# Four graph-attention layers over a sparse list: the order in which a group's rows and a dense block's heads are summed on TensorE

## The chip, the core and the metric

One NeuronCore of a Trainium2 chip runs the whole program; the other cores are idle. The metric is the device time of one execution in microseconds. Three executions of the kernel before took 2966.52, 2974.07 and 2981.21 us, median 2974.07.

A core has engines with queues of their own that meet only through semaphores: TensorE (PE; its loads of the stationary operand are listed as PEld), VectorE (DVE), ScalarE (ACT), GpSimd (POOL) and SyncE (SP, which here only issues DMAs). An instruction may carry an increment of its engine's semaphore, which happens when the instruction has ended, and instructions of other engines wait for a value of it.

## The reference

The input is 3327 nodes with 512 features in f32 and a symmetric adjacency matrix of about half a per cent density with a full diagonal. Four graph-attention layers follow each other, with 8, 4, 1 and 8 heads. Each is a normalization, a projection, a softmax over a node's neighbours and a weighted sum of their projected features, added to the node's own features. Layer 0, cut to its core:

```python
h = maximum(layernorm(x), 0)
v = (h @ W.T).reshape(n, H, d)                 # H heads of d = 512 / H columns
e = leaky_relu(e_src[:, None, :] + e_dst[None, :, :], 0.2)   # e_src, e_dst: v times two vectors a head
e = where(mask[:, :, None], e, -inf)
alpha = softmax(e, axis=1)
x = x + einsum('ijh,jhd->ihd', alpha, v).reshape(n, H * d)
```

Layers 1 and 2 put an ELU on the sum before they add it. All layers use the same adjacency.

## The kernel before

The nodes are padded to 26 tiles of 128. A first stage, the build, finds each node's neighbours (at most 40), sorts the nodes by degree and writes for each tile of 128 nodes (in order of degree) the indices of up to CAPS[t] neighbours, 36 for the first tile down to 11 for the last.

A layer then goes over its tiles, from the smallest degree to the largest. Tile t has CAPS[t] rows a node; they are taken in groups of up to four (GROUP). The rows are fetched by `Tile.fetch` (L836): POOL issues one indirect DMA for each row, which gathers 128 table rows of 528 values into a buffer g. There are five such buffers, so gathers run up to five groups ahead.

`Tile.scored` makes a group's weights on DVE (L893 and L895, or L915 and L917; in layer 0 with an exponential on ACT, L896). `Tile.group` multiplies and sums. For each row q of the group DVE writes the product of row and weights (L941), 128 by 512 f32, into row q of a buffer m; there are five of those. The tile's very first row is written straight into the tile's PSUM bank `po` instead. TensorE then adds the rows of m to the bank, one matmul with the identity for each (L946). An f32 matmul is two passes on TensorE, so each is two MATMUL and two LDWEIGHTS records. Layer 2 has one head and sums on DVE (L932 and L934), without these matmuls. Two banks `po` alternate between tiles.

When a tile's groups are done, its sum is divided (`means`, L964), up to four groups later, and added to x (L984), normalized (L992 to L1000), transposed on TensorE (L451), cut to positive values by ACT (L458), projected by TensorE (L469), and scaled and written to the next layer's table (L476 and L1031, a DMA from SP).

The first tiles, whose nodes have the most neighbours, are taken as dense blocks in layers 1, 2 and 3 (1, 9 and 3 tiles, DENSE): there all 26 tiles of source nodes are read in turn, with a mask. Layer 2's block is `Wholes` (L1192 is its matmul). Layers 1 and 3 use `Several`: for each of 52 units (two halves of the heads by 26 source tiles), SP loads features and mask (L1284, L1285), ACT makes ramps of the scores into PSUM (`weights`, L1298) and the scaled features vs of each of Q heads (`features`, L1309 and, for a last column, L1310), DVE adds and masks (L1314) and writes the weights e, and TensorE sums (`products`, L1332), one matmul for each of n tiles and Q heads: 2 in layer 1, 12 in layer 3. There are two buffers of e, two of vs, and one PSUM buffer of the ramps.

In `tile_gat_lists` all of this is put in an order by hand: a layer is a sequence of steps, one for each group, and each piece of work is put down with `later` for the start ("first"), the middle ("scored") or the end ("last") of a step. POOL, PE, DVE and ACT run their instructions in the order in which they are written. The framework adds the semaphores: an instruction waits only where it needs a value that its engine has not yet seen, and an increment is left off an instruction that nobody waits for (a later one then adds several at once).

The bank's sum does not depend on the order of its rows but for rounding, and the dense block's heads go to places of their own.

Of the kernel before, what the change touches and what calls it, by code (L numbers as in the profile page):

```python
# [374 lines left out]
def twice(ap, gap):  # L375

    return bass.AP(tensor=ap.tensor, offset=ap.offset,
                   ap=[list(ap.ap[0]), [gap, 2], list(ap.ap[-1])])
# [419 lines left out]
def tile_gat_lists(ctx: ExitStack, tc: tile.TileContext, x, adj, ws, avs, out, ident, half, slots, L, low, spare, mine, tabx, tabs):  # L798
# [7 lines left out]
    nc = tc.nc  # L806
# [40 lines left out]
    class Tile:  # L847
# [72 lines left out]
        def group(self, i):  # L920


            H, K, wt = HEADS[self.l], CAPS[self.t], self.wt
            D = F // H
            k0, n, g = self.groups[i]
            if H == 1:
                for q in range(n):
                    v = g[:, q, :].rearrange("p (s m) -> p s m", s=2)[:, :, :F // 2]
                    acc = self.po.rearrange("p (s m) -> p s m", s=2)
                    w = wt[:, k0 + q, 0:1]  # L930
                    if k0 + q == 0:
                        nc.vector.tensor_scalar(acc, v, w, None, OP.mult)  # L932
                    else:
                        nc.vector.scalar_tensor_tensor(acc, v, w, acc, OP.mult, OP.add)  # L934
                return
            m = pools["m"].tile([P, GROUP, F], F32, name="m")
            for q in range(n):
                v = g[:, q, :].rearrange("p (s m) -> p s m", s=2)[:, :, :F // 2]

                out_ = self.po if k0 + q == 0 else m[:, q, :]  # L940
                nc.vector.tensor_tensor(out_.rearrange("p (s h d) -> p s h d", s=2, d=D),  # L941
                                        v.rearrange("p s (h d) -> p s h d", d=D),
                                        wt[:, k0 + q, :H].rearrange("p (s h) -> p s h", s=2)
                                        .unsqueeze(3).to_broadcast([P, 2, H // 2, D]), OP.mult)
            for q in range(k0 == 0, n):
                nc.tensor.matmul(self.po, ident, m[:, q, :], start=False, stop=(k0 + q == K - 1),  # L946
                                 skip_group_check=True)

        def divisors(self):
# [176 lines left out]
    class Wholes:  # L1126
# [59 lines left out]
        def products(self, p, j):  # L1186
            e, v = self.e.pop((p, j)), self.v.pop((p, j))
            for q in range(3):
                tl = self.tiles[3 * p + q]
                if j == 0:  # L1190
                    tl.po = pools["w"].tile([P, BANK], F32, name="whole")
                nc.tensor.matmul(tl.po.rearrange("p (s m) -> p s m", s=2), e[:, q * P:(q + 1) * P],  # L1192
                                 v.rearrange("p (s m) -> p s m", s=2)[:, :, :F // 2],
                                 start=(j == 0), stop=(j == NT - 1))
# [51 lines left out]
    class Several:  # L1246
# [70 lines left out]
        def products(self, u):  # L1317

            Q, DV = self.Q, self.DV
            j, e, vs = u % NT, self.e[u % 2], self.vs[u % 2]  # L1320
            if j == 0:
                self.po = [pools["w"].tile([P, BANK], F32, name="whole") for _ in range(0, self.n * Q, self.per)]
                for o in self.po:
                    nc.tensor.matmul(o, ident, zero.to_broadcast([P, BANK]), start=True, stop=False,
                                     skip_group_check=True)
            for q in range(self.n):
                for h in range(Q):
                    o, o0 = self.where(q, h)
                    dst, mov = o[:, o0:o0 + DV], vs[:, h * DV:(h + 1) * DV]
                    if self.H == 8:  # L1330
                        dst, mov = twice(dst, self.per * DV - o0), twice(mov, (Q - h) * DV)
                    nc.tensor.matmul(dst, e[:, h, q * P:(q + 1) * P], mov, start=False, stop=(j == NT - 1),  # L1332
                                     skip_group_check=True)
# [169 lines left out]
```

## Time and profile before

| | us |
|---|---|
| median of three executions | 2974.07 |
| the profiled execution | 2992.93 |
| its span, from the first to the last instruction | 2991.2 |
| build (to the first matmul of L946) | 315 |
| layer 0 | 805 |
| layer 1 | 720 |
| layer 2 | 460 |
| layer 3 | 692 |

Mean granted TensorE clock: 0.862 of full speed. Busy shares over the span: PE 75%, PEld 42%, DVE 64%, ACT 31%, POOL 58%. The layers' times are stretches of the span between the first and the last matmul of L946 of each, rounded.

How to read the lines that follow. A group of instructions is its line, engine, operation, what it writes and reads with shapes, its count; then busy time and the mean of one in ns; then the idle time of the engine just before such instructions and what ended it. In a table of waits: who waited, for what; us in total, times, longest. "issue" is idle time in which the engine waited for nothing that the profile shows; "remote", in the chain "another core or an unknown queue", is a wait on a semaphore whose update the profile cannot put down to an instruction that ended shortly before. In a timeline: start, us, engine, line, operation, count, and in brackets the idle time before it.

Some of the other groups, for comparison:

| line, engine | what | count | mean ns |
|---|---|---|---|
| L836 POOL | one gather of 128 rows, by the second list of indices | 712 | 954 |
| L469 PE | projection of a tile, one pass | 1664 | 420 |
| L1192 PE | dense block of layer 2, one pass | 468 | 651 |
| L1314 DVE | add and mask, layer 3 | 35 of its kind | 1755 |
| L1309 ACT | features of one head, layer 3 | 136 of its kind | 338 |

### The profile page before, as it was taken

How to read it: one execution, taken by the hardware profiler on the slowest of the kernel's cores; microseconds unless marked ns; L12 is line 12 of the kernel's file. 1: busy time of each engine (PE TensorE's matmuls, PEld its weight loads, DVE VectorE, ACT ScalarE, POOL GpSimd, SP SyncE). 2: the span in 40 equal slices, each digit the busy share in tenths (PEclk: the TensorE clock that was granted, in tenths of full speed). 3: DMA queues.
4: the chain of work that ended last, by engine and by line, in shares of the span. 5: the costliest groups of instructions: out<-in, count | busy, mean ns of one | idle time of the engine just before them, and what ended most of it. 6: DMA issues, size and time to landing. Idle time of an engine off the chain costs nothing.

```text
span 2991.2 us, 26834 instructions
## 1 busy us (share of the span) xinstructions
PE 2235.0 (75%) x7082; PEld 1251.2 (42%) x7082; DVE 1901.9 (64%) x4831; ACT 919.9 (31%) x2363; POOL 1728.8 (58%) x1717
## 2 busy tenths in 40 slices
PE   4777687677677745788878787779785778777777
PEld 2665243343333322444434444345444445444443
DVE  7887656555555523776756655787776556656565
ACT  5782123322221111332222222343333333233230
POOL 7885455465456664565555552666664555545554
PEclk9888788888788877898888898989897888888889
DMA  6885477677676666676666664878765666656654
GB/s 229 308 288 170 136 223 212 183 233 219 184 208 188 199 179 180 189 206 185 201 207 188 195 188 122 248 242 260 222 215 148 192 189 189 178 169 183 182 171 137
DMA packets 258856, 594.16 MB, mean 199 GB/s; under 512 B 101827, under 2 KB 119235, under 8 KB 254342
## 3 DMA queue, kind: packets, MB, share of 16 engines
q0 software_dynamic: 124368, 432.13, 49.1%
q1 hardware_dynamic: 130582, 153.43, 16.3%
q10 hardware_dynamic: 3744, 6.82, 0.7%
q8 instruction: 57, 0.93, 0.1%
q14 instruction: 105, 0.86, 0.1%
HBM read 542.58 MB, written 49.65 MB: 198 GB/s over the span
## 4 chain that ended last, share of the span: by engine, by line
PE 28%; DVE 15%; issue 15%; another core or an unknown queue 8%; ACT 4%; POOL 3%; DMA 3%; SPq 0%; DVEq 0%; POOLq 0%; ACTq 0%
PE bank L946 17%; DVE m L941 6%; PE whole L1332 5%; PE pv L469 3%; POOL g L836 3%; PE whole L1192 2%; DVE bank L934 2%; DMA g<-tab,idxb 1%; DVE x L984 1%; DVE q L439 1%; DMA g<-tab,idxa 1%; DVE pw L917 1%; DMA ve<-tab 1%; DVE z L915 0%
## 5 line engine op out<-in xcount | busy, mean ns | idle before, releaser
L946 PE MATMUL bank<-m,ident 128*128 128x512 f32 x2414 | 1243.7, 661 | 279.9 <-issue 122.8
L836 POOL DMA_INDIRECT g<-tab,idxb x712 | 679.1, 954 | 488.0 <-issue 193.5
L946 PEld LDWEIGHTS bank<-m,ident 128*128 128x128 f32 x2414 | 490.0, 211 | 900.6 <-issue 602.0
L941 DVE TENSOR_TENSOR m<-g,pw 128x512 f32<-128x512 f32 x1207 | 751.9, 681 | 129.3 <-ACT pw L896 100.8
L469 PE MATMUL pv<-w,hT 128*128 128x264 f32 x1664 | 442.6, 420 | 101.5 <-ACT hT L458 48.0
L836 POOL DMA_INDIRECT g<-tabx,twiceb x342 | 324.0, 947 | 255.5 <-issue 159.8
L836 POOL DMA_INDIRECT g<-tab,idxa x297 | 283.2, 954 | 249.0 <-issue 80.8
L469 PEld LDWEIGHTS pv<-w,hT 128*128 128x128 f32 x1664 | 337.8, 207 | 206.7 <-issue 61.1
L1192 PE MATMUL whole<-ve,em 128*128 128x512 f32 x468 | 233.6, 651 | 54.7 <-DVE em L1165 34.8
L1332 PE MATMUL whole<-L,room 128*128 128x130 f32 x1248 | 172.1, 287 | 83.9 <-issue 83.6
L1332 PEld LDWEIGHTS whole<-L,room 128*128 128x128 f32 x1248 | 163.9, 201 | 115.5 <-issue 114.9
L696 POOL TENSOR_TENSOR key<-a,keys 128x3328 int32<-128x3328 int32 (+1 forms) x29 | 189.3, 6533 | 16.8 <-DVE cand L705 12.9
L934 DVE SCALAR_TENSOR_TENSOR bank<-g,L,bank 128x512 f32<-128x512 f32 x243 | 183.3, 754 | 10.7 <-issue 3.5
L1192 PEld LDWEIGHTS whole<-ve,em 128*128 128x128 f32 x468 | 94.4, 208 | 171.0 <-issue 104.6
L836 POOL DMA_INDIRECT g<-tabx,twicea x99 | 94.4, 954 | 118.7 <-issue 75.0
L1314 DVE SCALAR_TENSOR_TENSOR room<-r,low 128x1536 f32<-128x1536 f32 x35 | 61.4, 1755 | 136.2 <-issue 62.3
L451 PE MATMUL pt<-ident,xn 128*128 128x128 f32 x416 | 74.1, 297 | 98.2 <-issue 32.4
L705 DVE MAX8 cand<-key 128x8 f32<-128x208 int32 x416 | 144.1, 365 | 0.1
L896 ACT ACTIVATE pw<-z 128x32 f32<-128x32 f32 (+3 forms) x133 | 25.8, 194 | 303.9 <-DVE z L895 175.1
L1298 ACT ACTIVATE r<-low 128x128 f32<-128x128 f32 x104 | 38.6, 371 | 253.6 <-DVE low L1314 115.2
L1309 ACT ACTIVATE L<-spare 128x64 f32<-128x64 f32 x136 | 38.5, 338 | 237.5 <-remote 176.6
L451 PEld LDWEIGHTS pt<-ident,xn 128*128 128x128 f32 x416 | 56.1, 154 | 131.3 <-issue 63.0
(181 smaller groups left out, 2286.2 us busy)
## 6 DMA issues: line engine op xcount, KB each, us to landing
a<-in_adj SPq DMA_DIRECT2D x25, 1664.0 KB
tab<-v SPq DMA_DIRECT2D x78, 264.0 KB
ve<-tab SPq DMA_DIRECT2D x78, 264.0 KB
g<-tab SPq DMA_DIRECT2D x65, 264.0 KB
tabx<-vx SPq DMA_DIRECT2D x26, 528.0 KB
g<-tab,idxb POOLq DMA_INDIRECT x712
low<-tab SPq DMA_DIRECT2D x52, 132.0 KB
vx<-in_x ACTq DMA_DIRECT2D x26, 256.0 KB
```

The lines of the kernel that those rows point to most:

```text
L451: nc.tensor.transpose(pt[:, k, :], xn[:, k * P:(k + 1) * P], ident)
L469: nc.tensor.matmul(pv[:, s, :HF + 8], hT[:, k, :], W.w[:, k, s, :], start=(k == 0), stop=(k == KC - 1))
L696: nc.gpsimd.tensor_tensor(key[:, c:c + quarter], a[:, c:c + quarter], keys[:, c:c + quarter], OP.mult)
L705: nc.vector.max(cand[:, g * 8:(g + 1) * 8], key[:, g * SEG:(g + 1) * SEG])
L836: nc.gpsimd.indirect_dma_start(out=out_, out_offset=None, in_=table, in_offset=bass.IndirectOffsetOnAxis(ap=which, axis=0))
L934: nc.vector.scalar_tensor_tensor(acc, v, w, acc, OP.mult, OP.add)
L941: nc.vector.tensor_tensor(out_.rearrange("p (s h d) -> p s h d", s=2, d=D), v.rearrange("p s (h d) -> p s h d", d=D), wt[:, k0 + q, :H].re ...
L946: nc.tensor.matmul(self.po, ident, m[:, q, :], start=False, stop=(k0 + q == K - 1), skip_group_check=True)
L1192: nc.tensor.matmul(tl.po.rearrange("p (s m) -> p s m", s=2), e[:, q * P:(q + 1) * P], v.rearrange("p (s m) -> p s m", s=2)[:, :, :F // 2], ...
L1298: nc.scalar.activation(self.r[:, h, :], self.a[:, g, :], AF.Relu, bias=-1.0, scale=b[:, h:h + 1])
L1314: nc.vector.scalar_tensor_tensor(self.e[u % 2], self.r, 1.0, self.mk[u % 3].unsqueeze(1).to_broadcast([P, Q, n]), OP.add, OP.mult)
L1332: nc.tensor.matmul(dst, e[:, h, q * P:(q + 1) * P], mov, start=False, stop=(j == NT - 1), skip_group_check=True)
```

## The change

Two loops run backwards. In `Tile.group` the matmuls that add a group's rows to the bank begin with the row that DVE made last and end with the row that it made first; the mark for the last matmul of a tile (`stop`) moves with it. In `Several.products` the heads of each tile go from the last to the first. What is computed, and the number of instructions, stay.

```diff
@@ Tile.group
-            for q in range(k0 == 0, n):
-                nc.tensor.matmul(self.po, ident, m[:, q, :], start=False, stop=(k0 + q == K - 1),
+            first = int(k0 == 0)
+            for q in reversed(range(first, n)):
+                nc.tensor.matmul(self.po, ident, m[:, q, :], start=False, stop=(k0 + n == K and q == first),
                                  skip_group_check=True)
@@ Several.products
             for q in range(self.n):
-                for h in range(Q):
+                for h in reversed(range(Q)):
                     o, o0 = self.where(q, h)
                     dst, mov = o[:, o0:o0 + DV], vs[:, h * DV:(h + 1) * DV]
```

## The prediction

> **What bounds the kernel now.** I read the page's chain of waits first.
>
> ```profile
> PE 28%; DVE 15%; issue 15%; another core or an unknown queue 8%; ACT 4%; POOL 3%; DMA 3%; SPq 0%; DVEq 0%; POOLq 0%; ACTq 0%
> ```
>
> TensorE leads, but 8% of the span hangs on a releaser that the profile cannot name, and there is one core only. Next, busy time by stage (build, layers 0, 1, 2, 3; the edges are where the matmuls of L946 begin and end).
>
> ```profile
> 0.00:315.00 315.00, 210.17 (x838) 155.38 (x838) 247.41 (x1033) 181.03 (x381) 227.59 (x133) 0.87 0.69 238
> 315.00:1120.00 805.00, 570.44 (x1575) 282.47 (x1574) 439.56 (x1167) 182.92 (x543) 458.06 (x483) 0.82 0.68 200
> 1120.00:1840.00 720.00, 564.30 (x1583) 297.90 (x1584) 455.32 (x1199) 192.92 (x555) 386.04 (x407) 0.88 0.64 187
> 1840.00:2300.00 460.00, 354.84 (x1040) 198.62 (x1040) 348.73 (x649) 171.66 (x401) 290.01 (x307) 0.89 0.73 224
> 2300.00:2992.00 692.00, 535.29 (x2048) 316.80 (x2048) 410.90 (x784) 191.32 (x486) 367.13 (x387) 0.87 0.60 173
> ```
>
> Columns after the stage: PE, PEld, DVE, ACT, POOL busy, granted clock, DMA share, GB/s. Nobody passes 80% in layers 0, 1, 3, the three that the change touches. The groups:
>
> ```profile
> L946 PE MATMUL bank<-m,ident 128*128 128x512 f32 x2414 | 1243.7, 661 | 279.9 <-issue 122.8
> L941 DVE TENSOR_TENSOR m<-g,pw 128x512 f32<-128x512 f32 x1207 | 751.9, 681 | 129.3 <-ACT pw L896 100.8
> L1332 PE MATMUL whole<-L,room 128*128 128x130 f32 x1248 | 172.1, 287 | 83.9 <-issue 83.6
> ```
>
> Before L946 and L1332 TensorE idles 122.8 and 83.6 us for nothing that the profile shows. The waits say who suffers:
>
> ```profile
> ACT L L1309 <- remote: 233.0, 35, 17.3
> PEld bank L946 <- DVE m L941: 201.5, 206, 18.0
> PE bank L946 <- DVE m L941: 118.4, 39, 17.2
> ACT low L1309 <- remote: 94.7, 14, 16.4
> ACT v L476 <- remote: 89.0, 9, 18.6
> ```
>
> "remote" is the unnamed releaser. One such wait in the timeline:
>
> ```profile
> 2615.93 1.45 PE L946 MATMUL bank<-m,ident 128*128 128x512 f32 x3
> 2617.21 0.50 PE L1332 MATMUL whole<-L,room 128*128 128x130 f32 x3
> 2618.08 0.39 PE L1332 MATMUL whole<-L,room 128*128 128x130 f32 x2 [0.37 <-issue]
> 2618.80 0.27 PE L1332 MATMUL whole<-L,room 128*128 128x130 f32 x1 [0.33 <-issue]
> 2620.93 0.38 PE L1332 MATMUL whole<-L,room 128*128 128x130 f32 x2 [1.86 <-issue]
> 2621.66 0.33 PE L1332 MATMUL whole<-L,room 128*128 128x130 f32 x1 [0.34 <-issue]
> 2622.38 1.06 ACT L1309 ACTIVATE L<-spare 128x64 f32<-128x64 f32 x4 [12.79 <-remote]
> 2622.57 1.76 DVE L1314 SCALAR_TENSOR_TENSOR room<-r,low 128x1536 f32<-128x1536 f32 x1 [8.44 <-remote]
> ```
>
> ACT wants the products that TensorE ended at 2610.5. The trace's records of TensorE's semaphore tell the rest: 11 matmuls with an increment end between 2608.9 and 2615.7, one update is recorded before 2622.3 (at 2615.9), and then ten from 2622.36 to 2622.74, some 40 ns apart. TensorE's signals are held for up to 13 us, and towards the end TensorE itself trickles. In the build the 26 signals of L787 between 268.4 and 276.4 us, 0.2 to 0.5 us apart, are each recorded at once; from 284.3 on they are not (next update 289.0, then 297.3), and the first gather stands at 277.3. So I read: while POOL gathers, TensorE's increments drain slowly and a backlog forms.
>
> **Is it the number of signals?** Matmuls that carry an increment, counted in the trace: layer 0 525 (0.65 per us), layer 1 443 (0.62), layer 2 175 (0.38), layer 3 436 (0.63). The unnamed releaser's share of the chain in the same stages: 12.9%, 14.2%, 4.3%, 2.7%; in layer 3 TensorE itself is the chain (L946 38.7%, issue 25.1%, L1332 18.4%). Layer 2 has the largest gather traffic (DMA share 0.73), so gathers alone are not it; the build has 5.3 matmul and load records per us against layer 0's 3.9, so density is not it.
>
> **The change part by part.** No instruction, transfer or queue entry is added, removed or moved past another queue; only matmuls of one group swap places. (1) *Rows of a group.* DVE refills a buffer of m from its first row on, and each row now waits for the matmul that read it, so 883 of 1207 products signal. Summed backwards, the first refill waits for the group's last matmul, and the other rows for matmuls already known done: about one signal a group. The code makes 133, 118 and 105 groups, 356 in all. (2) *Heads.* ACT (L1309) rewrites head 0 first, which becomes the last matmul; 341 signals of L1332 fall to one for each of 104 units. New counts: layer 0 525-423+133=235 (0.29 per us), layer 1 443-271-102+118+52=240 (0.33), layer 3 436-239-186+105+52=168 (0.24). All lie under layer 2's 0.38.
>
> *Gain.* I let layers 0 and 1 fall to layer 2's share: (12.9-4.3)% of 805 = 69 us, (14.2-4.3)% of 720 = 71 us. In layer 3 TensorE's unexplained idle time, 83.6 before L1332 and 41.4 before L946 (waits of that stretch alone), shrinks as its signals, by 1-168/436=61%: 51+25=76 us. Together 216. Bounds: 0, if holding is no matter of counts; and all of it, 225 on the unnamed releaser in the three layers plus 206.4 before the two matmuls, 431, which the pace below cuts to 250. I take 216, from the stage that already runs at such a rate.
>
> *Cost.* A group's first matmul now waits for its last product. Four products of L941 take 2.48 us in the timeline, one 0.69, so a starved TensorE starts 1.79 us later; four matmul pairs then take 4x0.859 us (16 passes in 6.87) and are not starved again. Three layer ends cannot hide it: 3x1.79=5.4. In between, TensorE's own wait on L941 stands in 39 places: 0 to 39x1.79=70; I take half, 35, as L941 is 6% of the chain and L946 17%. Where TensorE is behind, DVE's rows are there already and the price is nothing; that backlog is the cover. Queued behind the waiting matmul are L451, L469 and L1332, and ACT's L458, L476, L1309 wait for those. DVE's refill waits 3x0.859=2.6 us longer than its first row did, five groups back; DVE waited on L946 for m 3.0 us in all, so 0, or 2.6 a group were those buffers short. ACT's first head waits 0.67 us longer (6 passes of L1332 at 0.112, 24 in 2.84) and ends as before: 0 to 35, I take 0, with ACT at 4% of the chain.
>
> Saturated streams of L946 run at 429 ns a pass with signals and without, so a signal costs no matmul time as such. [...]
>
> The granted clock, 0.82 in layer 0, could fall where TensorE idles longer before a burst. [...]
>
> *Sum.* 2991.2-216+5.4+35=2815.6 us of span; 1.7 around it, and the median lies 18.9 below the profiled 2992.93: 2798.
>
> **Rivals.** *The holding goes entirely.* The best 100 us of each layer shows the pace: 124 passes of L946 in layer 0 (900 to 1000), 136 in layer 1 (1200 to 1300), 109 in layer 3 (2600 to 2700). All 856, 838 and 720 passes at that pace take 690, 616, 661 us: 115, 104, 31 less, 250. 2991.2-250-17.2=2724; with the 76 above for layer 3, 2679. For it: the burst-like release looks like a queue, which under its rate stays empty. Against: layer 2 still shows 4.3%. *No effect.* The delay belongs to the gathers, each signal is late whatever their number, or the waits are hidden behind gathers (POOL needs 483x1.25=604 of layer 0's 805 us): 2974+5=2979. For it: the signals became late when gathers began. *Slower.* Holding stays and TensorE's later start is paid at all 39 places on the chain, 70+5.4: 2974+75=3049. It decides once the gain is under 75 us. For it: 201.5 us of weight loads wait for L941. Against: means come up to four groups later, there are five m buffers and two banks.
>
> **How the numbers follow.** Forecast 0.50 (own range 2763, with 216 gained at 5.4 paid, to 2909, with 140 gained at 75 paid), entire 0.22, no effect 0.14 (0.03 faster, 0.08 same, 0.03 slower), slower 0.14. A measurement here tells about 0.5% (15 us) from no change. Faster 0.75, same 0.08, slower 0.17. The range 2680 to 2985 leaves out the slower cases and a little below.
>
> **What would show it.** Of L946's products some 356 carry an increment; ACT's waits on "remote" fall from 233.0, 94.7 and 89.0 to under half; the unnamed share of layers 0 and 1 falls to 4 to 5%; idle before L1332 falls under 40 us; waits of L946 on L941 grow, to 120 to 190 for the matmul. I am wrong if increments fall by half and the "remote" waits stand, or if TensorE's wait on L941 grows by over 200 us.

## The result, and the profile after

| | us |
|---|---|
| kernel before, median of 19 executions | 2973.98 |
| changed kernel, median of 19 executions | 2997.03 |
| ratio, with its 95% interval | 1.0081 (1.0059 to 1.0104) |
| changed kernel, profiled execution, and its span | 3004.1, 3002.3 |

The changed kernel is slower by 0.8%, some 23 us; the forecast was 2798. The built program does what the diff says: of 1748 matmuls that carried an increment 950 are left, for the rows 271 of 883 and for the heads 157 of 341. By layer that is 248, 189 and 163 in layers 0, 1 and 3, against 525, 443 and 436.

The chain of waits of the changed kernel, and its groups (idle time before the group and what ended most of it stand last; the code's lines are one further down from L946 on, so L947 sums the rows and L1333 the heads):

```profile
PE 24%; DVE 14%; issue 14%; another core or an unknown queue 8%; POOL 5%; DMA 3%; ACT 3%; DVEq 0%; POOLq 0%; ACTq 0%; SPq 0%
...
L947 PE MATMUL bank<-m,ident 128*128 128x512 f32 x2414 | 1243.0, 662 | 302.0 <-DVE m L941 163.1
...
L1333 PE MATMUL whole<-L,room 128*128 128x130 f32 x1248 | 181.1, 291 | 98.7 <-issue 97.9
```

The unnamed releaser still has 8% of the span in the chain. (The chain can't be followed to the start: it breaks off at 681 us in the profile before and at 873 us in this one.) Idle time without a named cause before the heads went up, 83.6 to 97.9 us. What ended most of the idle time before the rows is a new one: the product, 163.1 us. The waits (total us, times, longest):

```profile
ACT L L1310 <- remote: 230.7, 21, 17.9
...
PE bank L947 <- DVE m L941: 163.1, 56, 18.1
...
ACT low L1310 <- remote: 103.4, 11, 17.7
...
ACT v L476 <- remote: 85.0, 10, 20.7
```

All three "remote" rows stand where they stood (233.0, 94.7, 89.0). Summed over all instructions of ScalarE and VectorE, such waits are 788 us before and 791 us after in layers 0, 1 and 3. Sorted by the semaphore whose update ended them, over the whole span, 665 us before and 732 after waited for TensorE and 134 and 76 for VectorE: the increments that come late are not TensorE's alone. TensorE's wait on the product is 44.7 us longer in this trace than in the one before, 56 waits instead of 39. Busy time by stage (PE, PEld, DVE, ACT, POOL, granted clock, DMA share, GB/s):

```profile
310.00:1126.00 816.00, 574.42 (x1591) 285.78 (x1591) 443.22 (x1175) 183.03 (x549) 460.19 (x484) 0.83 0.67 198
1126.00:1853.00 727.00, 562.22 (x1549) 291.44 (x1548) 449.87 (x1189) 189.10 (x543) 385.89 (x406) 0.86 0.64 185
...
2340.00:3003.00 663.00, 521.07 (x1976) 308.69 (x1976) 408.79 (x777) 181.45 (x469) 360.79 (x379) 0.87 0.61 178
```

The clock is about what it was in the three layers (0.82, 0.88, 0.87); over the span it is 0.861 after 0.862. The last row's 663 us can't be set against the 692 before: its window begins 11 us ahead of layer 3's first row sum, the one before began 33 us ahead. From that row sum to the end of the span it is 651 us after 658, and from layer 0's first row sum to it 2041 after 2017: in this pair of profiles the loss lies ahead of layer 3.

### The profile page after: what moved, and what is told of

It reads as the page before. It is cut to its first block, busy times and chain, and to the rows that moved or that the text cites. A ratio compares the mean times of both kernels' runs of the same rounds, so it can differ in the third digit from the quotient of the medians.

```text
span 3002.3 us, 26833 instructions
## 1 busy us (share of the span) xinstructions
PE 2235.3 (74%) x7082; PEld 1251.4 (42%) x7082; DVE 1904.0 (63%) x4831; ACT 914.8 (30%) x2363; POOL 1732.4 (58%) x1717
## 4 chain that ended last, share of the span: by engine, by line
PE 24%; DVE 14%; issue 14%; another core or an unknown queue 8%; POOL 5%; DMA 3%; ACT 3%; DVEq 0%; POOLq 0%; ACTq 0%; SPq 0%
PE bank L947 14%; DVE m L941 6%; PE whole L1333 4%; POOL g L836 4%; PE pv L469 3%; DVE bank L934 2%; PE whole L1193 2%; DMA g<-tab,idxb 1%; DMA g<-tab,idxa 1%; DVE x L985 1%; DMA ve<-tab 1%; DVE z L915 1%; DVE pw L917 0%; DVE q L439 0%
## 5 line engine op out<-in xcount | busy, mean ns | idle before, releaser
L947 PE MATMUL bank<-m,ident 128*128 128x512 f32 x2414 | 1243.0, 662 | 302.0 <-DVE m L941 163.1
L947 PEld LDWEIGHTS bank<-m,ident 128*128 128x128 f32 x2414 | 492.2, 212 | 918.0 <-issue 680.4
L941 DVE TENSOR_TENSOR m<-g,pw 128x512 f32<-128x512 f32 x1207 | 751.7, 681 | 173.5 <-ACT pw L896 143.9
L1333 PE MATMUL whole<-L,room 128*128 128x130 f32 x1248 | 181.1, 291 | 98.7 <-issue 97.9
L1333 PEld LDWEIGHTS whole<-L,room 128*128 128x128 f32 x1248 | 166.9, 203 | 133.5 <-issue 132.7
L1159 ACT ACTIVATE r<-low,mc,ve 128x384 f32<-128x384 f32 x78 | 52.6, 674 | 181.6 <-DVE em L1166 69.5
L476 ACT ACTIVATE v<-pv,root 128x528 f32<-128x528 f32 x78 | 53.9, 691 | 174.2 <-remote 85.0
```

Source lines behind the costliest of these rows:

```text
L476: nc.scalar.activation(v.rearrange("p (s n) -> p s n", s=2), pv[:, :, :ROW // 2], AF.Copy, scale=rstd)
```

## The experiments

**One part at a time.** The two hunks of the diff alone: rows without heads (first), heads without rows (second).

```diff
-            for q in range(k0 == 0, n):
+            for q in reversed(range(first, n)):
...
-                for h in range(Q):
+                for h in reversed(range(Q)):
```

> Only the rows of a group are summed from the last one on; the heads of the dense block keep their order. Theory A (the first matmul of a group now waits for the group's last product instead of its first, and TensorE pays for that wherever it has nothing else queued: its wait on the product grew by 45 us from before to after, of which about half reaches the end): +0.5 to +1.0% over before, that is the whole of what the change costs; TensorE's increments for the row sums about 270 as after. Rival B (the heads carry the cost, because layer 3's unnamed share of the chain rose from 18 to 37 us): within 0.3% of before. Rival C (the increments themselves are worth something and the heads give it back): faster than before by 0.5% or more.

> Only the heads of the dense block are summed from the last one on; the rows keep their order. Theory A (late start of the row groups): within 0.3% of before, although the increments of the dense products fall from 341 to about 157. Rival B (the heads carry the cost): +0.5 to +1.0%. Theory of the forecast (increments are what holds the signals back): faster by about 2% (76 us were put on layer 3, most of it on these products).

Rows: 2997.33 us against 2978.95, +0.68% (0.34 to 1.03). Heads: 2979.45, +0.12% (-0.15 to 0.40), though the heads' increments fell from 341 to 158. So the whole cost is in the rows, and theory B and the forecast's gain are out. The waits of the kernel with the rows alone:

```profile
ACT L L1310 <- remote: 219.6, 41, 17.9
...
PE bank L947 <- DVE m L941: 161.8, 54, 18.6
```

ScalarE's unnamed wait is hardly shorter. The wait on the product is the changed kernel's, but this row scatters: with the rows in their old order it was 118.4 in the kernel before and is 138.2 in the kernel with the heads alone. The times show the cost; one trace each doesn't.

**Late, or descending?** Two kernels separate them. The heads keep their order in both. The first sums a group as last, first, second, third. The second makes and sums the products of every other group from the last to the first (the gathers are turned in the groups between), so that TensorE starts each group at its first product and the increments stay at 1748.

```diff
+            order_ = [n - 1, *range(k0 == 0, n - 1)]
...
+            made = list(range(k0 == 0, n))
+            if next(turns):
+                made.reverse()
```

> The change, but with the rows of a group summed as last, first, second, third: TensorE begins a group as late as after, and the rows behind the first carry no wait at all either. Theory A (the late start is the cost): as slow as after, +0.5 to +1.0% over before. Rival D (the descending order itself, the last tile read first and the first tile freed last, is the cost): nearer to before, within 0.3%.

> Kernel before, but every second group has its products made, and its rows summed and fetched, from the last to the first: TensorE begins each group at its first product, as before, and waits as often as before. Theory A (late start is the cost): within 0.3% of before. Rival E (the order in which rows are read matters by itself): slower or faster by over 0.5%.

Late: 2995.84, +0.72% (0.47 to 0.96). Alternating: 2981.68, +0.05% (-0.22 to 0.32). The cost comes with the wait for the group's last product, not with a direction (rivals D and E fall). It is a net cost: the late kernel, like the one with the rows alone, also has fewer increments (1140), and no run starts late with all of them or early with few. What the rows' fewer increments are worth by themselves stays unmeasured.

**Which groups pay?** Only the last group of each tile backwards, and (with k0 + n < K in the condition) all groups but the last.

```diff
+            if k0 + n == K:
+                rows_ = rows_[::-1]
```

> Kernel before, with only the last group of each tile summed from the last row on; the groups before it in ascending order. Theory A1 (lateness counts only where a tile ends, where normalisation and projection wait for the last row): the whole cost of the rows, +0.5 to +0.8%. Theory A2 (lateness counts at every group for which TensorE waits): under +0.3%, since most groups are left as before.

> Kernel before, with all groups but the last of each tile summed from the last row on. Theory A1: within 0.3% of before. Theory A2: +0.4 to +0.8%.

These ran on another chip, and there the kernel before takes 2427.32 us, not 2979: the same program takes 18.5% less. The kernel with the last groups backwards, 2427.86, is +0.04% (-0.05 to 0.12); all but the last, 2430.40, is +0.12% (0.01 to 0.22). Here what cost there is sits in the middle groups, not at the tile ends (A1 falls, and A2's 0.4 to 0.8% isn't reached); on a chip like the first these two weren't measured. The larger finding is the chip. The experiments ran on five: on three (numbers 8, 4 and 7) the kernel before takes 2978.95, 2954.84 and 2977.33 us, on two (1 and 12) 2427.32 and 2428.41. So the change itself was run once more, and fell on chip 12, with its parts beside it:

> The changed kernel once more, since the runs so far came from two chips: on the first the kernel before takes 2979 us with waits of ScalarE and VectorE for no named releaser, on the second 2427 us without any such wait. Theory A2 (lateness at groups for which TensorE waits): +0.5 to +1.0% on the first chip; on the second +0.1 to +0.3%, since there summing all groups but the last from the end took +0.12%. Rival S (on the chip without held signals the saved increments come through as a gain): faster by over 0.3% on the second.

> Rows alone from the last on, once more. Theory A2: as the changed kernel, within 0.2% of it, on either chip. Rival S: on the second chip faster than before.

> All groups but the last of a tile from the last row on, once more. Theory A1 (only tile ends count): within 0.3% of before on the first chip. Theory A2: +0.4 to +0.8% on the first chip, +0.1 to +0.2% on the second.

As A2 expected on such a chip, the whole change takes 2435.42 us, +0.29% (0.17 to 0.42), the rows alone +0.25% (0.13 to 0.38), all but the last groups +0.17% (0.08 to 0.26). The changed kernel on this chip, its chain, a group and its waits:

```profile
DVE 20%; DMA 20%; PE 16%; POOL 10%; issue 10%; ACT 4%; DVEq 0%; SPq 0%; POOLq 0%; ACTq 0%
...
L947 PE MATMUL bank<-m,ident 128*128 128x512 f32 x2414 | 1127.0, 614 | 151.4 <-DVE m L941 146.2
...
L1333 PE MATMUL whole<-L,room 128*128 128x130 f32 x1248 | 147.8, 274 | 0.0
```

```profile
ACT L L1310 <- PE whole L1333: 56.7, 29, 5.3
...
ACT v L476 <- PE pv L469: 41.3, 11, 5.7
...
ACT low L1310 <- PE whole L1333: 8.6, 11, 1.7
```

There is no unnamed releaser here, neither in the chain nor in a single wait. These waits of ScalarE name the matmul and last under 6 us. TensorE's idle time without a named cause, summed over all its groups, is 6.7 us; in the traces above it was 304.7 before and 270.4 after. The same 950 increments, the same gathers, and nothing is held: the holding isn't in the program alone. And where nothing is held, saving 798 increments brings no net gain either (rival S falls).

**Is TensorE's own queue the cause?** The guess (theory H) was that TensorE's instructions run far ahead into a long queue, and that its increments are late for that. So a drain, meant to let TensorE's next instruction start only when the ones before have ended, was put at each step of the layer's loop (587 of them); a second kernel has more, in transpositions and projections. In the trace below a drain is recorded until 753.71 us, and the next matmul starts at 753.77.

```diff
+                nc.tensor.drain()
                 do("first")
```

> Kernel before, with one drain of TensorE at each step of a layer's loop: TensorE's sequencer can't run ahead of the array by more than a step. Nothing of the computation changes. Theory H (increments are held when TensorE's own queue is long and dense, not because there are many of them): the waits of ScalarE and VectorE with no named releaser (799 us summed over the stages before) fall by more than half, TensorE's trickle (251 us) too, and the time falls by 1 to 5% less what 500 drains cost, 50 to 100 ns each. Rival G (the gathers or the profiler hold them, whatever TensorE does): both sums stay, and the time rises by 0.5 to 2%.

> As the kernel with a drain at each step, with drains also behind each transposition and each quarter of a projection, so that no more than 18 matmuls stand between two drains, and mostly 2 to 4. Theory H: the holds that were left with one drain a step, those in the projections, go as well; the summed waits with no named releaser under 200 us. Rival G: the sums stay at about 800 and 250 us, and the time rises by 1 to 4%.

> One drain of TensorE a step, once more. On the second chip, where nothing is held, 587 drains cost 1.2% (29 us, 49 ns each), and it should show that again. On the first chip theory H (a long dense queue of TensorE is what holds its increments) expects the waits without a named releaser (799 us) and the trickle (251 us) to fall by more than half and the time by 1 to 5%; rival G (they are held whatever TensorE does) leaves both sums within a quarter and adds 0.5 to 2% to the time.

> One drain of TensorE a step. On the second chip +1.0 to +1.3% as twice before. On the first chip, theory H: waits without a named releaser (799 us before) and trickle (251 us) fall by more than half, time down by 1 to 5%; rival G: both sums within a quarter of before, time up by 0.5 to 2%.

The first three of these ran on chips that hold nothing and give the drains' bare price: +1.23% and +1.00% (28.7 us on chip 1, 49 ns each; the 50 to 100 ns of the first expectation were the author's guess, ahead of any run), and +3.78% with the finer ones. The fourth ran on chip 4, which holds: 3100.47 against 2954.84, +5.2% (4.6 to 5.8), 248 ns a drain. Its waits:

```profile
PE bank L946 <- issue: 346.1, 55, 20.4
...
ACT L L1309 <- remote: 162.0, 27, 15.2
```

A drained TensorE stands for up to 20 us for no cause that the profile names. The longest of these in the timeline (start, us, engine, line; idle time before it in brackets), TensorE's rows, then two each of ScalarE's, VectorE's and POOL's:

```profile
729.67 3.72 PE L469 MATMUL pv<-w,hT 128*128 128x264 f32 x16
753.77 2.92 PE L946 MATMUL bank<-m,ident 128*128 128x512 f32 x3 [20.38 <-issue]
```

```profile
737.64 0.21 ACT L899 ACTIVATE idxb<-g 128x4 int32<-128x4 f32 x1
752.33 0.70 ACT L476 ACTIVATE v<-pv,root 128x528 f32<-128x528 f32 x1 [14.49 <-remote]
```

```profile
741.92 0.18 DVE L893 TENSOR_TENSOR z<-g,pw 128x32 f32<-128x32 f32 x1
747.41 0.19 DVE L895 SCALAR_TENSOR_TENSOR z<-z 128x32 f32<-128x32 f32 x1 [5.32 <-remote]
```

```profile
752.01 0.95 POOL L836 DMA_INDIRECT g<-tabx,twiceb  x1 [0.30 <-issue]
753.26 0.94 POOL L836 DMA_INDIRECT g<-tabx,twiceb  x1 [0.30 <-issue]
```

The projection ends at 733.39. TensorE then has nothing under way; its drain is recorded from 728.83 to 753.71, the next matmul starts at 753.77, and the increment for the projection at 752.31, 18.9 us after the work was done. ScalarE starts at 752.33. VectorE is held too, and by itself: L895 waits for nothing but VectorE's own L893, which ended at 742.10, and starts at 747.41. Theory H falls: a bounded, even an empty queue is held as well. Unnamed waits of ScalarE and VectorE fell from 799 us (in the first trace of the kernel before) to 529, but TensorE's idle time for no named cause rose from 304.7 to 527.6, the 346.1 us before L946 among it (122.8 before): together 1104 and 1056. TensorE's shortest such gaps, under 3 us, did shrink, from 237 to 61 us, but all of them under 10 us, the trickle of 251 us in the expectations, came to 307. The hold moved into the drains, and the time rose. Rival G fits better, though not by its numbers: the first sum fell by a third rather than staying within a quarter, and 5.2% is over its 0.5 to 2%.

What else happens from 733 to 754? POOL issues a gather every 1.25 us, without a break. In the trace of the kernel before, waits of over 3 us that ScalarE or VectorE has for no named releaser end 2 to 5 us after such a run of gathers (gaps of under 0.7 us counted as none) in 44 cases of 73; of their other long waits 69 of 245 do, and 16% of the time lies there. In the changed kernel it is 47 of 74, with the rows alone 47 of 81. So holds and runs of gathers tend to end close together. That is an association: POOL in its turn waits for VectorE (216.8 us for L915 alone in the drained kernel's trace), so that a hold can also end a run of gathers, and the hold shown above ended at 752.31, before its run of gathers did (754.20). No run changes the gathers alone, so that they cause the holds is not shown.

**Does the price grow with the lateness?** Rows of two groups summed together, from the last one on: up to seven products late instead of three, and 195 waits of the row sums instead of 356. The rows alone and the heads ran beside it for the second time, on a chip that holds.

```diff
+            self.held = (self.held if i % 2 else []) + [(m, q, k0 + q) for q in range(n) if k0 + q]
+            if i % 2 or k0 + n == K:
+                for m_, q, k in reversed(self.held):
```

> Rows of two groups summed together, from the last row of the second group on: TensorE's first matmul waits for up to eight products instead of four, that is up to seven products late instead of three, and increments for the rows fall to about one for two groups. Theory A2, cost in proportion to the lateness: 7/3 of what rows alone took, +0.5 to +0.7% on the second chip, +1.4 to +1.9% on the first. Rival (only that the groups' overlap with DVE is lost, once): as rows alone, +0.2 to +0.3% on the second chip. Theory of the forecast (increments are the price): faster than rows alone.

> Two groups summed together from the last row on. Cost in proportion to the lateness: 7/3 of the rows' run beside it (+0.5 to +0.8% where nothing is held). Cost paid once, whatever the lateness: as the rows' run, within 0.15%. Increments pay for the lateness: below the rows' run by more than that, which would show only on a chip with held increments.

> Rows of a group alone from the last on, beside the two kernels below on one chip. Theory A2: +0.4 to +1.0% on a chip with held increments, +0.2 to +0.35% on one without.

> Heads of the dense block alone, once more. Theory A2 (all of the cost is the late start of the rows' groups): within 0.1% of before on the second chip, where rows alone took +0.25% and the whole change +0.29%; within 0.3% on the first. Rival S (fewer increments gain where none are held): faster by over 0.1% on the second chip.

> Heads alone. If the two parts add up: within 0.1% of before where nothing is held (rows +0.25%, the whole change +0.29%). On a chip with held increments the two measurements so far are +0.12% [-0.15, +0.40] and -0.33% [-0.61, -0.05]; a small gain from the increments expects about -0.2% again, none expects 0.

| | chip 8 | chip 4 | chip 7 |
|---|---|---|---|
| rows alone | +0.68% (0.34 to 1.03) | | +0.67% (0.37 to 0.98) |
| two groups at once | | +0.40% (0.15 to 0.66) | +0.22% (-0.15 to 0.58) |
| heads alone | +0.12% (-0.15 to 0.40) | -0.33% (-0.61 to -0.05) | -0.08% (-0.37 to 0.22) |

Twice the lateness doesn't cost twice; on chip 7 it costs less than the single dose by 0.45 points, where a price in proportion expected 1.6%. TensorE's wait on the product with two groups at once (chip 7, then chip 4) and with the rows alone (chip 7):

```profile
PE bank L948 <- DVE m L941: 174.1, 49, 18.1
```

```profile
PE bank L948 <- DVE m L941: 209.3, 49, 17.5
```

```profile
PE bank L947 <- DVE m L941: 172.0, 62, 17.5
```

The waits are fewer and longer. Their sum on chip 7 is that of the rows alone beside it, on chip 4 it is larger, and the heads alone, with the rows in their old order, have 165.6 there and 129.0 on chip 7: the sum of this wait doesn't tell the price. The number of increments doesn't explain the difference: 1175 are left here and 1140 with the rows alone. The heads are 0.10% faster in the mean of three. The interval of chip 4 excludes zero, those of the two others don't: a gain of one to three tenths of a per cent is neither shown nor excluded, while the 2% that the forecast expects of them is excluded.

## Why the prediction was wrong

*The counts* held: 235, 240 and 168 increments were expected in layers 0, 1 and 3, 248, 189 and 163 were left. The two parts were less exact: 271 of the rows' instead of 356, 157 of the heads' instead of 104.

*The gain is the step that failed*: "I let layers 0 and 1 fall to layer 2's share", and in layer 3 the idle time to shrink "as its signals". That read a rate of increments as the cause of the holding from four stages in which rate and holding happened to go together. The increments fell by 53, 57 and 63%, and the unnamed waits went from 236, 225 and 327 us to 297, 176 and 319. In layer 1, which the chain covers in both profiles, the unnamed share came to 12.4%, not 4 to 5%; in layer 3 TensorE's two idle terms, 83.6 and 41.4 us, came to 97.9 and 18.0, 9 us less instead of 76. Nothing of the 216 us is seen at the end. On two other chips nothing is held at 1748 increments (with drains) or 950, and with the drain an increment was held for 18.9 us with none behind it from TensorE. The prediction had the contrary evidence at hand: late signals set in when the first gather was issued. It dropped the gathers since layer 2 has the most traffic and hardly any holds. It also misread layer 0: the chain breaks off at 681 us, so the 12.9% of 805 us are 104 us in layer 0's last 439 alone. What holds the increments, and why layer 2 is spared on the chips that hold, stays open.

*The cost* was right in kind and twice too large: 5.4 and 35 us were put on the late start, and the rows alone took 20 us twice (0.68% of 2979, 0.67% of 2977), net of whatever their fewer increments gained. TensorE's wait on the product, expected at 120 to 190 us, came out at 163.1, but with the rows in their old order it lies anywhere from 118.4 to 165.6 in four traces, so that this hit says little. On the chips without holds it is 6 us (0.25% of 2428). The rule behind "39 waits by 1.79 us", a price in proportion to lateness and to the number of waits, isn't borne out: with two groups at once it fell. What decides how much of such a wait reaches the end stays open.

*DVE's refill and ACT's first head* at zero: nothing contradicts it. The heads alone moved the time by 0.1% in the mean.

*The rivals.* "No effect" was right that signals are late whatever their number (788 us of unnamed waits in layers 0, 1 and 3 with 1748 increments in all, 791 with 950; that the delay belongs to the gathers isn't shown) but took 5 us for the late start, and the result lies 18 us above it. "Slower" had the mechanism of the loss, at 75 us instead of 20. "The holding goes entirely" is out. The prediction's own condition for being wrong, increments by half and "remote" waits unmoved, is what happened; its other one, a wait on L941 longer by over 200 us, is not.

*Fewer increments by themselves.* No run shows a gain: where nothing is held the change lost 0.29%. None excludes a small one either, since the rows' cost is net and the heads alone took +0.12, -0.33 and -0.08% in three runs.

*The granted clock* stood in the prediction as a possible loss and not in its sum. In the kernel before it was 1.00 from 1080 to 1094 us and 0.50 from 1121 to 1124, behind a gap of TensorE of 26.59 us. The change added no such loss in the mean: 0.861 after 0.862 over the span.

## What to carry to other kernels

Fewer semaphore increments brought no gain that these runs could show. What ScalarE waited for in the drained kernel was the arrival of one increment, 18.9 us after the work that it stood for. Summing from the last-made row on gives up the overlap of producer and consumer within a group, and here that cost 0.7% on chips with held increments (0.68 and 0.67%, chips 8 and 7), 0.25% on one without (chip 12). Before a stall is put down to a count, change the count alone: the heads' hunk by itself would have shown in one run that its increments are not worth the 2% put on them. And before the share of a chain is multiplied by a stage, see whether the chain reaches back over that stage.

## What the runs showed of the hardware

One program takes 2955 to 2979 us on three chips and 2427 to 2428 us on two. Windows of the changed kernel on chip 12 (its layers 0, 1 and 3), columns as above, show the difference in the clock and in the DMA share:

```profile
307.00:958.00 651.00, 541.79 (x1648) 279.49 (x1648) 457.39 (x1209) 193.07 (x577) 470.86 (x497) 0.93 0.85 259
958.00:1507.00 549.00, 504.91 (x1562) 274.47 (x1562) 445.14 (x1174) 190.50 (x544) 383.88 (x405) 0.97 0.79 241
...
1950.00:2433.00 483.00, 459.36 (x1976) 277.97 (x1976) 405.00 (x771) 174.21 (x454) 354.14 (x373) 0.99 0.79 240
```

DVE, ACT and POOL are busy for about as long as in the changed kernel's first trace (in layer 0 457, 193 and 471 us; there 443, 183 and 460). TensorE's clock is 0.93 to 0.99 instead of 0.83 to 0.87, the DMA share 0.79 to 0.85 instead of 0.61 to 0.67, and layer 3 takes 483 us from its first row sum to the end instead of 651.

The chips also differ in the trace itself. Counted in it, an execution leaves 17,904 records of semaphore updates before and 17,878 after on the chips that hold, and 42,940 of the changed kernel on chip 12. Of TensorE's increments 1430 of 1748 have a record before; on chip 12 all 950 do. So part of what reads "remote" may be an update that was never recorded; but the waits themselves are real, since ScalarE started when the late update came (752.33 us after 752.31 in the drained kernel). Whether the recording itself holds the engines on those chips no run here shows, since every trace read here is of a recorded execution; nor was it tried whether shorter bursts of gathers would end the holds.
